# Routed rows turned in 32-blocks on VectorE instead of transposed on TensorE

## The chip, the cores and the metric

The kernel runs on one core of one Trainium2 chip. The time is that of the device for one execution, in microseconds. The program was executed three times for its times before, and once more under the profiler.

## The reference, cut to what matters

The reference is two layers, each a mixing part multiplied by the SiLU of a mixture-of-experts part, with a residual. The first layer is a RWKV recurrence with a two-expert mixture, the second a pooled attention with two shared and sixteen routed experts, four of them per token. All is float32, with T = 2048 tokens of D = 512. The change touches the second mixture:

```python
def _moe_forward(u, shared_w1, shared_b1, shared_w2, shared_b2, routed_w1, routed_b1, routed_w2, routed_b2, centroids, bias):
    flat = u.reshape(-1, d)                                   # 2048 x 512, already normalized
    h = jax.nn.relu(jnp.einsum('td,ndf->ntf', flat, shared_w1) + shared_b1[:, None, :])
    shared_out = jnp.einsum('ntf,nfd->td', h, shared_w2) + shared_b2.sum(0)
    out = flat + shared_out
    scores = jax.nn.sigmoid(flat @ centroids.T) + bias
    vals, idx = jax.lax.top_k(scores, KR)                     # KR = 4 of 16
    gating = jnp.zeros_like(scores).at[jnp.arange(T)[:, None], idx].set(vals)
    gating = gating / jnp.clip(gating.sum(-1, keepdims=True), 1e-08)

    def step(acc, ew):
        w1, b1, w2, b2, g = ew                                # 512 x 352, 352 x 512
        hj = jax.nn.relu(flat @ w1 + b1)
        yj = hj @ w2 + b2
        return (acc + yj * g[:, None], None)
    rout, _ = jax.lax.scan(step, rout0, (routed_w1, routed_b1, routed_w2, routed_b2, gating.T))
    return (out + rout).reshape(b, s, d)
```

## The kernel before

**Rows are sorted by expert through DRAM.** The normalized token rows of the second layer are kept in SBUF in `acc` ([128, 16, 544] by token tile: 512 values and 32 columns of gates and token numbers). They are written at L861 and transposed at L865 (by TensorE, with a copy on ScalarE) into `xT`, from which the routing scores `pl` (L870) come; `largest` and `chosen` pick the experts. 64 scatters on GpSimd's queue (L1043) then write every row of `acc` four times into the DRAM buffer `xs`, grouped by expert and padded to tiles of 128 rows. There are at least 64 such tiles and at most 80 (`NRT`); with these inputs 74 go through `hidden_rows`. Meanwhile the shared experts are computed (L956, L1105); their result plus the row itself (the add at L1111) is stored into two DRAM buffers, `comb[0]` and `comb[1]`, each holding half of the 512 columns.

**A routed tile has two functions.** `hidden_rows(j)` (L1657) loads the four weight pieces of the tile's expert with `load1` (L659 w1, 704 KB; L660 w2, 512 KB; L661 w3, 192 KB; L662 a bias row), from a pool of three buffers, and the tile x, [128, 544], in one DMA (L1671) that comes after all 64 scatters. The product needs the columns of x on the partitions: four TensorE transposes write `tp` in PSUM (L1678, pool `m1t` of one buffer), ScalarE copies it to `xg` (L1680), and 12 products `ph` follow (L1685), whose ReLU goes to `hT` (L942). VectorE takes the gate `g` (L1693) and the destination row `to` (L1698, L1703) from the last 32 columns of x. `down_rows(j)` (L1706) multiplies `hT` by w2, w3 (`py`, L1709, two PSUM buffers), VectorE scales by the gate to y (L1714, four buffers), and two scatter-adds on GpSimd's queue (L1717) accumulate the halves of y in `comb`.

**The loop** (L1747 to L1767) issues `hidden_rows(j)`, then pieces of the attention of the second layer as `attend_by(j)` deals them out, then `down_rows(j-1)`. All weight, x and attention loads go through SP's queue. From tile 65 on each turn stands under a test of the number of tiles. A scheduler in the framework decides the order of the instructions of each engine from this; the program's order is only its input. Attention uses the PSUM pool `aps` of three buffers (L1319). After the loop the sums are loaded from `comb` (y<-comb), put through SiLU, multiplied by attention's result, added to the residual and stored.

Of the kernel before, what the change touches and what calls it, by code (L numbers as in the profile page):

```python
# [9 lines left out]
F32 = mybir.dt.float32  # L10
I32 = mybir.dt.int32
AF = mybir.ActivationFunctionType
ALU = mybir.AluOpType
AX = mybir.AxisListType
PSUM = bass.MemoryType.PSUM
AFTER = mybir.DependencyInfo(mybir.DependencyClass.Sync, mybir.DependencyReason.DATA)

P = 128
T = 2048
D = 512  # L20
NT = T // P
NC = D // P
# [39 lines left out]
NR = 16  # L62
# [5 lines left out]
NF1 = len(FCH)  # L68
NRT = T * KR // P + NR
DX = D + 32  # L70


def bc(ap, axis, shape):
# [4 lines left out]
def tile_kernel(ctx: ExitStack, tc: tile.TileContext, a: dict):  # L78
    nc = tc.nc
# [4 lines left out]
    ident = const.tile([P, P], F32, name="ident")  # L84
# [23 lines left out]
    xs = dram.tile([NRT * P, DX], F32, name="xs")  # L108
# [66 lines left out]
    for i in range(0, NT, 2):  # L175
        xin = n0.tile([P, 2, D], F32, tag="xin", bufs=NT // 2, name="xin")
        nc.sync.dma_start(
            out=xin, in_=a["x"][i * P : (i + 2) * P, :].rearrange("(n p) d -> p n d", p=P)
# [10 lines left out]
        out=wdc, in0=gate0_w[:, :, 1], in1=gate0_w[:, :, 0], op=ALU.subtract  # L189
# [35 lines left out]
    for i in range(0, NT, 2):  # L225
# [6 lines left out]
        for j in range(2):  # L232
            xn = xin[:, j, :]
# [52 lines left out]
    own = run[:, 0, NT - 1 : NT]  # L286
# [367 lines left out]
    def load1(pool, e, pick, row):  # L654

        w1 = pool.tile([P, NC, F1], F32, tag=f"w1{e}", name="w1")
        w2 = pool.tile([P, NF1 - 1, D], F32, tag=f"w2{e}", name="w2")
        w3 = pool.tile([P, D], F32, tag=f"w3{e}", name="w3")
        nc.sync.dma_start(out=w1, in_=pick(a["w1"]))  # L659
        nc.sync.dma_start(out=w2, in_=pick(a["w2"])[:, 0 : NF1 - 1, :])  # L660
        nc.sync.dma_start(out=w3[0:last, :], in_=pick(a["w2"])[0:last, NF1 - 1, :])  # L661
        nc.sync.dma_start(out=w3[last : last + 1, :], in_=row(a["b2"]))  # L662
        return w1, w2, w3
# [184 lines left out]
    for b in range(NRB):  # L848
        rows2 = slice(b * RB, (b + 1) * RB)
        xr = tr.tile([P, n, D], F32, tag="xr", name="xr")  # L850
        nc.sync.dma_start(out=xr, in_=a["x"][rows2, :].rearrange("(n p) d -> p n d", p=P))
        i0 = b * n
        for s in range(n):
            nc.vector.tensor_tensor(
                out=xr[:, s, :], in0=xr[:, s, :], in1=acc[:, i0 + s, 0:D], op=ALU.add
            )
        nc.sync.dma_start(out=xr1[rows2, :].rearrange("(n p) d -> p n d", p=P), in_=xr)
        mv, rstd = norm_stats(xr, n)
        for s in range(n):
            i = i0 + s  # L860
            nc.vector.tensor_scalar(  # L861
                out=acc[:, i, 0:D], in0=xr[:, s, :], scalar1=mv[:, s, 0:1],
                scalar2=rstd[:, s : s + 1], op0=ALU.subtract, op1=ALU.mult,
            )
            transposed(m1y, acc[:, i, :], xT[:, :, i * P : (i + 1) * P], "py")  # L865
        if (i + 1) % (TB // P) == 0:
            t0 = i + 1 - TB // P
            pl = m1y.tile([NR, TB], F32, tag="py", name="pl")
            for c in range(NC):
                nc.tensor.matmul(  # L870
                    out=pl, lhsT=cent[:, c, :], rhs=xT[:, c, t0 * P : (i + 1) * P],
                    start=(c == 0), stop=(c == NC - 1),
                )
# [225 lines left out]
    def down_shared(tb, hT):  # L1099
        for s in range(TB // P):  # L1100
            t = tb * (TB // P) + s
            py = m1y.tile([P, D], F32, tag="py", name="py")
            for e, w in enumerate(ws):
                for f, n in enumerate(rows_of):
                    nc.tensor.matmul(  # L1105
                        out=py, lhsT=hT[0:n, e, f, s * P : (s + 1) * P],
                        rhs=down(w, f, n), start=(e == 0 and f == 0),
                        stop=(e == NS - 1 and f == NF1 - 1),
                    )
            y = m1s.tile([P, D], F32, tag="y", bufs=3, name="y")  # L1110
            nc.vector.tensor_tensor(out=y, in0=py, in1=acc[:, t, 0:D], op=ALU.add)  # L1111
            for h, c_ in enumerate(comb):
                nc.sync.dma_start(
                    out=c_[t * P : (t + 1) * P, :], in_=y[:, h * D // 2 : (h + 1) * D // 2]
                )
# [200 lines left out]
    logps.close()  # L1316


    aps = ctx.enter_context(tc.tile_pool(name="aps", bufs=3, space=PSUM))  # L1319
    QB = 256  # L1320

    def softmax(s, heads, keys, neg, wt=None, last=True):
# [206 lines left out]
    sh.close()  # L1529


    m1t = ctx.enter_context(tc.tile_pool(name="m1t", bufs=1, space=PSUM))
    aq = ctx.enter_context(tc.tile_pool(name="aq", bufs=1))
    aq2 = ctx.enter_context(tc.tile_pool(name="aq2", bufs=2))
    fin = ctx.enter_context(tc.tile_pool(name="fin", bufs=NT // 2))
# [118 lines left out]

    FIRST = 3

    def hidden_rows(j):  # L1657
        e = nc.values_load(
            tile_e[0:1, j : j + 1], engines=[mybir.EngineType.SP], min_val=0, max_val=NR - 1,
            skip_runtime_bounds_check_because="it is a count of at most NR, cut at NR - 1",  # L1660
        )
        def weights():
            return load1(
                m1w, "", lambda t: t[bass.ds(e, 1)].rearrange("e p c f -> p (e c) f"),
                lambda t: t[bass.ds(e, 1), :],
            )

        if j < FIRST:
            w = weights()
        x = m1x.tile([P, DX], F32, tag="x", bufs=4, name="x")  # L1670
        got = nc.sync.dma_start(out=x, in_=xs[j * P : (j + 1) * P, :])  # L1671
        for name in sent:
            tc.add_manual_dep(got.ins, name, AFTER, reason="any of them may hold its rows")
        if j >= FIRST:
            w = weights()
        tp = m1t.tile([P, NC, P], F32, tag="tp", name="tp")
        for c in range(NC):
            nc.tensor.transpose(tp[:, c, :], x[:, c * P : (c + 1) * P], ident)  # L1678
        xg = m1x.tile([P, NC, P], F32, tag="xg", name="xg")
        nc.scalar.copy(xg, tp)  # L1680
        hT = hts[j % len(hts)]
        for f, n in enumerate(FCH):
            ph = m1ps.tile([P, P], F32, tag="ph", name="ph")
            for c in range(NC):
                nc.tensor.matmul(  # L1685
                    out=ph[0:n, :], lhsT=up(w, f, n, c), rhs=xg[:, c, :],
                    start=(c == 0), stop=(c == NC - 1),
                )
            relu(hT[0:n, f, :], ph[0:n, :], b1t[0:n, j, f : f + 1])

        junk = m1x.tile([P, NR], F32, tag="junk", name="junk")
        g = m1x.tile([P, 1], F32, tag="g", name="g")
        nc.vector.tensor_tensor_reduce(  # L1693
            out=junk, in0=x[:, D : D + NR], in1=oh[:, j, :], scale=1.0, scalar=0.0,
            op0=ALU.mult, op1=ALU.add, accum_out=g,
        )

        nc.vector.scalar_tensor_tensor(  # L1698
            out=junk[:, 0:1], in0=x[:, D + NR + 1 : D + NR + 2], scalar=away[:, 1:2],
            in1=x[:, D + NR : D + NR + 1], op0=ALU.mult, op1=ALU.add,  # L1700
        )
        to = m1x.tile([P, 1], I32, tag="to", bufs=6, name="to")
        nc.vector.tensor_tensor(out=to, in0=junk[:, 0:1], in1=away[:, 0:1], op=ALU.add)  # L1703
        return w, hT, g, to
# [28 lines left out]
    def parts_by(j):  # L1733
# [2 lines left out]
            return (j + 1) * (PARTS - LATE) // FULL_TILES  # L1736
        return PARTS - LATE + (j - FULL_TILES) * LATE // MAYBE

    pending, taken = None, 0

    def attend_by(j):
# [5 lines left out]
    for j in range(NRT + 1):  # L1747

        with contextlib.ExitStack() as more:
            if j > FULL_TILES:  # L1750
                more.enter_context(tc.If(held > j - 1))
            made = hidden_rows(j) if j < NRT else None
            if j <= FULL_TILES:
                attend_by(j)
            if pending is not None:
                down_rows(*pending)
            pending = (j, *made) if made is not None else None
            i = j - (FULL_TILES - NT)
            if 0 <= i < NT and i % 2 == 0:
                xo = fin.tile([P, 2, D], F32, tag="xo", name="xo")  # L1760
                nc.sync.dma_start(
                    out=xo, in_=xr1[i * P : (i + 2) * P, :].rearrange("(n p) d -> p n d", p=P)
                )
                rest_of[i] = xo
        if j > FULL_TILES:
            attend_by(j)
# [119 lines left out]
```

## Time and profile before

| | us |
|---|---|
| median of three runs | 1950.14 (1944.71 to 1953.96) |
| profiled execution | 1940.83 |
| its span | 1939.1 |
| routed stage, first x load to last scatter-add landed | 1347.4 to 1877.0 |
| busy: PE, VectorE, ScalarE, GpSimd | 1857.2, 787.3, 532.9, 465.9 |

The groups of the routed stage, from the page's list of costliest groups. A row gives the line, the engine, the operation, what is written and read, the shape and the count; then the busy time in us and the mean of one in ns; then the engine's idle time just before them, and what ended most of it. PEld is the loading of the stationary operand, which lies beside the products.

```profile
L1685 PE MATMUL ph<-xg,w 128*128 128x128 f32 (+1 forms) x1776 | 214.4, 277 | 1.5 <-DMA w<-in_w_dram 1.5
L1709 PE MATMUL py<-w,ht 128*128 128x512 f32 (+1 forms) x438 | 209.1, 593 | 0.0
...
L1678 PEld LDWEIGHTS tp<-ident,x 128*128 128x128 f32 x296 | 36.7, 140 | 38.8 <-issue 21.5
```

A float32 product appears as two entries on PE: 24 for the 12 products of `ph`, 6 for the 3 of `py`.

### The profile page before, as it was taken

What the parts mean: (1) busy time and instruction counts of PE and PEld (TensorE: products, weight loads), DVE (VectorE), ACT (ScalarE), POOL (GpSimd) and SP (SyncE); (2) the same over time, 40 slices, a digit from 0 to 9 for tenths busy, and PEclk for the clock granted to TensorE, in tenths of its full rate; (3) what the DMA queues carried; (4) which work ended last, traced back from release to release, by engine and by line L of the source; (5) the groups of instructions that cost most, each with busy time, mean ns of one, the idle gap of its engine ahead of it and who ended that gap; (6) DMA issues with size and microseconds to landing.
All of it is one profiled execution on the core that took longest, in us unless ns stands there. A gap on an engine that the chain in (4) does not pass through costs nothing.

```text
span 1939.1 us, 23212 instructions
## 1 busy us (share of the span) xinstructions
PE 1857.2 (96%) x8107; PEld 1292.1 (67%) x8107; DVE 787.3 (41%) x1565; ACT 532.9 (27%) x994; POOL 465.9 (24%) x350
## 2 busy tenths in 40 slices
PE   5899999999999999999989999999999999999977
PEld 4677777787877777777533654444767777777654
DVE  8713627272634545252166544331323232223116
ACT  6212322232323232232134212221222222222223
POOL 1301212121201111020210453000344444444430
PEclk9799999999999999999999999999999999999998
DMA  7548685635654443436461553022999999999963
GB/s 250 205 144 278 205 306 178 221 108 163 197 195 141 130 131 125 157 98 233 147 227 46 174 215 114 31 95 87 313 290 316 320 311 298 292 282 265 299 148 131
DMA packets 214096, 381.35 MB, mean 197 GB/s; under 512 B 16972, under 2 KB 134476, under 8 KB 213080
## 3 DMA queue, kind: packets, MB, share of 16 engines
q1 hardware_dynamic: 183896, 332.78, 50.7%
q0 software_dynamic: 28784, 45.63, 10.7%
q10 hardware_dynamic: 1296, 1.41, 0.3%
q8 instruction: 67, 1.10, 0.2%
q14 instruction: 53, 0.43, 0.1%
HBM read 294.04 MB, written 85.72 MB: 196 GB/s over the span
## 4 chain that ended last, share of the span: by engine, by line
PE 83%; DMA 6%; DVE 3%; issue 2%; POOL 2%; ACT 2%; SPq 0%; POOLq 0%; ACTq 0%; DVEq 0%
PE pg L571 23%; PE py L593 12%; PE ph L1685 9%; PE py L1709 9%; PE proj L416 7%; PE py L1105 4%; PE ph L956 3%; PE pw L1593 2%; DMA comb<-y,to 2%; PE pq L1352 2%; PE tp L1678 1%; PE po L712 1%; PE ps L1560 1%; PE pl L870 1%; PE pw L1477 1%
## 5 line engine op out<-in xcount | busy, mean ns | idle before, releaser
L571 PE MATMUL pg<-xg,w 128*128 128x256 f32 (+1 forms) x2304 | 497.8, 369 | 3.3 <-ACT xg L563 3.3
L571 PEld LDWEIGHTS pg<-xg,w 128*128 128x128 f32 x2304 | 420.9, 191 | 95.0 <-issue 42.1
L1717 POOL DMA_INDIRECT comb<-y,to x146 | 226.9, 1554 | 300.0 <-DMA comb<-y,to 222.2
L593 PE MATMUL py<-wd,hT 128*128 128x512 f32 x544 | 256.9, 593 | 2.9 <-DVE hT L578 2.9
L1685 PEld LDWEIGHTS ph<-xg,w 128*128 128x128 f32 (+1 forms) x1776 | 201.9, 182 | 39.8 <-ACT xg L1680 32.9
L1685 PE MATMUL ph<-xg,w 128*128 128x128 f32 (+1 forms) x1776 | 214.4, 277 | 1.5 <-DMA w<-in_w_dram 1.5
L1709 PE MATMUL py<-w,ht 128*128 128x512 f32 (+1 forms) x438 | 209.1, 593 | 0.0
L578 DVE TENSOR_TENSOR hT<-sg,pg 128x256 f32<-128x256 f32 (+1 forms) x144 | 57.0, 402 | 338.4 <-ACT sg L576 338.3
L576 ACT ACTIVATE sg<-pg 128x256 f32<-128x256 f32 (+1 forms) x144 | 53.5, 372 | 419.7 <-PE pg L571 419.4
L593 PEld LDWEIGHTS py<-wd,hT 128*128 128x128 f32 x544 | 102.1, 190 | 72.2 <-issue 61.9
L1714 DVE TENSOR_SCALAR y<-py,g 128x512 f32<-128x512 f32 x73 | 54.6, 749 | 206.7 <-PE py L1709 196.1
L942 ACT ACTIVATE ht<-ph,b1t 128x128 f32<-128x128 f32 (+1 forms) x222 | 81.3, 366 | 178.9 <-PE ph L1685 161.4
L1709 PEld LDWEIGHTS py<-w,ht 128*128 128x128 f32 (+1 forms) x438 | 75.1, 191 | 49.8 <-issue 49.3
L1680 ACT COPY xg<-tp 128x512 f32<-128x512 f32 x74 | 43.4, 586 | 177.2 <-PE tp L1678 166.4
L1105 PE MATMUL py<-w,hT 128*128 128x512 f32 (+1 forms) x192 | 89.3, 596 | 0.0
L956 PE MATMUL ph<-xT,w 128*128 128x512 f32 (+1 forms) x192 | 88.0, 597 | 0.0
L1043 POOL DMA_INDIRECT xs<-acc,slot x64 | 63.1, 985 | 67.2 <-DMA xs<-acc,slot 43.5
L1352 PE MATMUL pq<-xT,wqg 128*128 128x256 f32 x224 | 56.6, 401 | 14.2 <-DVE wide L1572 9.6
L712 PE MATMUL po<-wo,yb 128*128 128x512 f32 x128 | 59.3, 620 | 9.6 <-ACT acc L721 5.5
L416 PE MATMUL proj<-xm,wr 128*128 128x256 f32 x256 | 60.9, 393 | 5.6 <-ACT v L452 5.6
L464 POOL TENSOR_TENSOR ex<-st_p,qt 128x1024 f32<-128x1024 f32 x8 | 18.3, 2288 | 193.0 <-DVE qt L463 193.0
L1678 PEld LDWEIGHTS tp<-ident,x 128*128 128x128 f32 x296 | 36.7, 140 | 38.8 <-issue 21.5
(418 smaller groups left out, 2180.9 us busy)
## 6 DMA issues: line engine op xcount, KB each, us to landing
w<-in_w_dram SPq DMA_DIRECT2D x76, 704.0 KB
w<-in_w_dram SPq DMA_DIRECT2D x76, 512.0 KB
w<-in_w_gate_dram SPq DMA_DIRECT2D x72, 512.0 KB
w<-in_w_up_dram SPq DMA_DIRECT2D x72, 512.0 KB
wd<-in_w_down_dram SPq DMA_DIRECT2D x72, 512.0 KB
xs<-zero SPq DMA_DIRECT2D x16, 1360.0 KB
x<-xs SPq DMA_DIRECT2D x74, 272.0 KB
w<-in_w_dram SPq DMA_DIRECT2D x76, 192.0 KB
```

Source lines behind the costliest of these rows:

```text
L416: nc.tensor.matmul(out=ps[:, j, :], lhsT=w_[:, c, (o0 + j) * P : (o0 + j + 1) * P], rhs=xm[:, c, :], start=(c == 0), stop=(c == NC - 1),)
L571: nc.tensor.matmul(out=pg[:, i, 0:n], lhsT=w[:, c, i * FH + f * P : i * FH + (f + 1) * P], rhs=xg[:, c, 0:n], start=(c == 0), stop=(c == N ...
L593: nc.tensor.matmul(out=p, lhsT=hT[:, u * P : (u + 1) * P], rhs=wd[:, f, :], start=first_, stop=last_,)
L712: nc.tensor.matmul(out=po, lhsT=yb[:, c, s * P : (s + 1) * P], rhs=wo[:, c, :], start=(c == 0), stop=(c == NC - 1),)
L942: nc.scalar.activation(dst, src, AF.Relu, bias=b)
L956: nc.tensor.matmul(out=ph[0:n, :], lhsT=up(w, f, n, c), rhs=xT[:, c, cols], start=(c == 0), stop=(c == NC - 1),)
L1043: ins = nc.gpsimd.indirect_dma_start(out=xs, out_offset=bass.IndirectOffsetOnAxis(ap=slot[:, i, k : k + 1], axis=0), in_=acc[:, i, :], in_ ...
L1105: nc.tensor.matmul(out=py, lhsT=hT[0:n, e, f, s * P : (s + 1) * P], rhs=down(w, f, n), start=(e == 0 and f == 0), stop=(e == NS - 1 and f ...
L1352: nc.tensor.matmul(out=pq[:, j, :], lhsT=w[:, c, w0 : w0 + P], rhs=xT[:, c, tc0], start=(c == 0), stop=(c == NC - 1),)
L1685: nc.tensor.matmul(out=ph[0:n, :], lhsT=up(w, f, n, c), rhs=xg[:, c, :], start=(c == 0), stop=(c == NC - 1),)
L1709: nc.tensor.matmul(out=py, lhsT=hT[0:n, f, :], rhs=down(w, f, n), start=(f == 0), stop=(f == NF1 - 1),)
L1717: nc.gpsimd.indirect_dma_start(out=c_, out_offset=bass.IndirectOffsetOnAxis(ap=to, axis=0), in_=y[:, h * D // 2 : (h + 1) * D // 2], in_of ...
```

## The change

The transposition of a routed tile on TensorE, its PSUM buffer and ScalarE's copy are replaced by one VectorE transpose of 32 x 32 blocks. That instruction turns each of the 4 x 16 blocks of a [128, 512] tile within its 32 partitions; it doesn't move a block to other partitions. So the blocks are put on their partitions by the load: the quarter q (32 partitions) of the tile gets, from each of four groups of 32 rows, the column blocks that belong to q. For each of these to be one run of 128 values in DRAM, the columns of the rows are stored in another order: 512 columns as (c q k), with k of 32, are kept in `acc` and `xs` as (q c k).

- At L861 the row goes to a tile `xn` of its own (two buffers), is transposed from there, and ScalarE copies it reordered to `acc`. The shared experts' add reads `acc` through a permuted view.
- `weights(j)` and `rows_in(j)` are split from `hidden_rows(j)`. `rows_in` loads x in four DMAs of 32 partitions each and the last 32 columns as `own` in a fifth, and turns them. It is called one tile ahead; the weights of three tiles are called before the first.
- `aps` has four buffers instead of three, `m1t` is gone.

```diff
@@ the rows of the second layer @@
+            xn = tr.tile([P, D], F32, tag="xn", bufs=2, name="xn")
             nc.vector.tensor_scalar(
-                out=acc[:, i, 0:D], in0=xr[:, s, :], scalar1=mv[:, s, 0:1],
+                out=xn, in0=xr[:, s, :], scalar1=mv[:, s, 0:1],
                 scalar2=rstd[:, s : s + 1], op0=ALU.subtract, op1=ALU.mult,
             )
-            transposed(m1y, acc[:, i, :], xT[:, :, i * P : (i + 1) * P], "py")
+            transposed(m1y, xn, xT[:, :, i * P : (i + 1) * P], "py")
+            nc.scalar.copy(
+                acc[:, i, 0:D].rearrange("p (c q k) -> p q c k", q=NB, k=BL),
+                xn.rearrange("p (c q k) -> p q c k", q=NB, k=BL),
+            )
...
-            nc.vector.tensor_tensor(out=y, in0=py, in1=acc[:, t, 0:D], op=ALU.add)
+            nc.vector.tensor_tensor(
+                out=y.rearrange("p (c q k) -> p c q k", q=NB, k=BL),
+                in0=py.rearrange("p (c q k) -> p c q k", q=NB, k=BL),
+                in1=acc[:, t, 0:D].rearrange("p (q c k) -> p c q k", q=NB, k=BL), op=ALU.add,
+            )
...
-    aps = ctx.enter_context(tc.tile_pool(name="aps", bufs=3, space=PSUM))
+    aps = ctx.enter_context(tc.tile_pool(name="aps", bufs=4, space=PSUM))
...
-    m1t = ctx.enter_context(tc.tile_pool(name="m1t", bufs=1, space=PSUM))
...
-    def hidden_rows(j):
+    def weights(j):
...
+        return load1(
+            m1w, "", lambda t: t[bass.ds(e, 1)].rearrange("e p c f -> p (e c) f"),
+            lambda t: t[bass.ds(e, 1), :],
+        )
...
-        x = m1x.tile([P, DX], F32, tag="x", bufs=4, name="x")
-        got = nc.sync.dma_start(out=x, in_=xs[j * P : (j + 1) * P, :])
...
-        tp = m1t.tile([P, NC, P], F32, tag="tp", name="tp")
-        for c in range(NC):
-            nc.tensor.transpose(tp[:, c, :], x[:, c * P : (c + 1) * P], ident)
+    def rows_in(j):
+        x = m1x.tile([P, NB, NC, BL], F32, tag="x", bufs=4, name="x")
+        own = m1x.tile([P, DX - D], F32, tag="own", bufs=4, name="own")
+        mine = xs[j * P : (j + 1) * P, :]
+        loads = [
+            nc.sync.dma_start(
+                out=x[q * BL : (q + 1) * BL].rearrange("p b c k -> p b (c k)"),
+                in_=mine[:, q * P : (q + 1) * P].rearrange("(b r) k -> r b k", r=BL),
+            )
+            for q in range(NB)
+        ]
+        loads.append(nc.sync.dma_start(out=own, in_=mine[:, D:]))
...
         xg = m1x.tile([P, NC, P], F32, tag="xg", name="xg")
-        nc.scalar.copy(xg, tp)
+        nc.vector.transpose(xg.rearrange("p c (b r) -> p b c r", r=BL), x)
+        return xg, own
+
+    def hidden_rows(j, w, xg, own):
...
+    ready = [weights(j) for j in range(FIRST)]
+    rows = rows_in(0)
...
-            made = hidden_rows(j) if j < NRT else None
+            made = None
+            if j < NRT:
+                mine, rows = rows, rows_in(j + 1) if j + 1 < NRT else None
+                made = hidden_rows(j, ready.pop(0) if ready else weights(j), *mine)
```

`NB` is 4 and `BL` is 32. The gate and the destination read `own` where they read the last columns of x before.

More of the change, by code (lines that the diff above doesn't have):

```diff
@@ L70 @@
 DX = D + 32
+NB = 4
+BL = P // NB
 def bc(ap, axis, shape):
@@ L860, in tile_kernel @@
             i = i0 + s
+            xn = tr.tile([P, D], F32, tag="xn", bufs=2, name="xn")
             nc.vector.tensor_scalar(
-                out=acc[:, i, 0:D], in0=xr[:, s, :], scalar1=mv[:, s, 0:1],
+                out=xn, in0=xr[:, s, :], scalar1=mv[:, s, 0:1],
                 scalar2=rstd[:, s : s + 1], op0=ALU.subtract, op1=ALU.mult,
             )
-            transposed(m1y, acc[:, i, :], xT[:, :, i * P : (i + 1) * P], "py")
+            transposed(m1y, xn, xT[:, :, i * P : (i + 1) * P], "py")
+            nc.scalar.copy(
+                acc[:, i, 0:D].rearrange("p (q c k) -> p q c k", q=NB, k=BL),
+                xn.rearrange("p (c q k) -> p q c k", q=NB, k=BL),
+            )
         if (i + 1) % (TB // P) == 0:
@@ L1661, in hidden_rows @@
         )
[L1662 to L1665, printed above, removed]
-            )
-        if j < FIRST:
-            w = weights()
-        x = m1x.tile([P, DX], F32, tag="x", bufs=4, name="x")
-        got = nc.sync.dma_start(out=x, in_=xs[j * P : (j + 1) * P, :])
[L1672 to L1675, printed above, removed]
-        tp = m1t.tile([P, NC, P], F32, tag="tp", name="tp")
-        for c in range(NC):
-            nc.tensor.transpose(tp[:, c, :], x[:, c * P : (c + 1) * P], ident)
+        return load1(
[10 more added lines that the diff above has]
+                in_=mine[:, q * P : (q + 1) * P].rearrange("(b r) k -> r b k", r=BL),
+            )
+            for q in range(NB)
+        ]
+        loads.append(nc.sync.dma_start(out=own, in_=mine[:, D:]))
+        for got in loads:
+            for name in sent:
+                tc.add_manual_dep(got.ins, name, AFTER, reason="any of them may hold its rows")
         xg = m1x.tile([P, NC, P], F32, tag="xg", name="xg")
-        nc.scalar.copy(xg, tp)
+        nc.vector.transpose(xg.rearrange("p c (b r) -> p b c r", r=BL), x)
+        return xg, own
+    def hidden_rows(j, w, xg, own):
         hT = hts[j % len(hts)]
@@ L1693, in hidden_rows @@
         nc.vector.tensor_tensor_reduce(
-            out=junk, in0=x[:, D : D + NR], in1=oh[:, j, :], scale=1.0, scalar=0.0,
+            out=junk, in0=own[:, 0:NR], in1=oh[:, j, :], scale=1.0, scalar=0.0,
             op0=ALU.mult, op1=ALU.add, accum_out=g,
@@ L1698, in hidden_rows @@
         nc.vector.scalar_tensor_tensor(
-            out=junk[:, 0:1], in0=x[:, D + NR + 1 : D + NR + 2], scalar=away[:, 1:2],
-            in1=x[:, D + NR : D + NR + 1], op0=ALU.mult, op1=ALU.add,
+            out=junk[:, 0:1], in0=own[:, NR + 1 : NR + 2], scalar=away[:, 1:2],
+            in1=own[:, NR : NR + 1], op0=ALU.mult, op1=ALU.add,
         )
```

## The prediction, on record before the changed kernel ran

> **What bounds the kernel now.** I read the busy shares by slice first, then the same by windows of 50 us over the routed stage, then its waits, then the packets. The busy tenths put the stage in the second half of the span, where PE and DMA both stand at 9:
>
> ```profile
> span 1939.1 us, 23212 instructions
> ...
> PE   5899999999999999999989999999999999999977
> ...
> DMA  7548685635654443436461553022999999999963
> ...
> L1717 POOL DMA_INDIRECT comb<-y,to x146 | 226.9, 1554 | 300.0 <-DMA comb<-y,to 222.2
> ...
> L1680 ACT COPY xg<-tp 128x512 f32<-128x512 f32 x74 | 43.4, 586 | 177.2 <-PE tp L1678 166.4
> ```
>
> In the windows (PE, PEld, DVE, ACT, POOL busy; then clock, DMA share, GB/s) PE has no idle time at all, and the DMA share is also about 1; DVE and ACT are idle three quarters of the time:
>
> ```profile
> 1500.00:1550.00 50.00, 50.00 (x276) 35.15 (x275) 12.99 (x45) 13.82 (x33) 21.29 (x14) 1.00 1.05 323
> ...
> 1750.00:1800.00 50.00, 50.00 (x264) 34.25 (x263) 13.31 (x44) 13.54 (x31) 23.58 (x16) 1.00 0.90 254
> ```
>
> So two resources are near their limits. Which is the nearer? The waits from 1400 to 1860 say: the weight loads on SP wait for PE to release buffers, hardly for transfers: in the order of limits PE comes first. But the scatter-adds wait for one another throughout, and VectorE waits for them:
>
> ```profile
> SPq L660 <- PE py L1709: 166.7, 57, 6.6
> ...
> SPq L660 <- DMA w<-in_w_dram: 6.6, 7, 1.5
> ```
>
> ```profile
> POOL comb L1717 <- DMA comb<-y,to: 201.3, 87, 5.5
> ...
> DVE to L1703 <- DMA comb<-y,to: 101.5, 30, 6.7
> ```
>
> Reading single instructions, the first product of the stage starts at 1355.5, the last y ends at 1859.4, and the last scatter-add lands at 1877.0: the accumulation runs 17 us behind the products. Where no attention work lies between (tiles 64 to 70) the y follow each other 5.81 us apart; the mean over tiles 6 to 63 is 7.07.
>
> **The change, part by part.**
>
> 1. *Four transposes and their copy go.* Each PE transpose costs 0.107 us when they run together, 0.43 us a tile, with some 0.13 us of entry and a slower first product of the group: 5.81 − (2.66 ph + 2.58 py) = 0.57 us. Over 74 tiles PE is relieved of **42 us**. ACT loses 74 × 0.586 = 43 us, worth nothing: it is busy 27%.
>
> 2. *VectorE gets 75 block transposes* of 128x512 f32. No such row is in the trace; the nearest are whole-tile VectorE operations, 0.69 us (L1111, L839) and 0.749 us (L1714). I bound it by 0.6 and 1.2 us and take 0.75: 56 us, on an engine with 35 us free of each 50. The transposition of tile j+2 follows y(j) in VectorE's order. Its wait is for x(j+2), issued about two tiles, over 10 us, before; loads of x landed 6.27 us (median) after issue. So it costs 0; if the cover fails, what is queued behind it is to(j+2) and y(j+1), hence the scatter-add, and py's two PSUM buffers, which stop PE one tile later.
>
> 3. *One x load becomes four of 64 KB and one of 16 KB.* Packets: 128 of 2176 B become 512 of 512 B and 128 of 128 B, with 64 more semaphore writes. In the trace's packet records 2176 B takes 88 ns, 512 B 27 ns (the xnt loads, L245), 128 B 13 ns, a semaphore 9 ns. So 11.3 us of engine time become 13.8 + 1.7 + 0.6 = 16.1: **+0.30 us a tile** over 16 engines. All of a tile's DMAs together now need 93.9/16 = 5.87 us (weights 56.1, x 11.5, scatter-adds 26.3), so 6.17 after. With some 17 us of attention's loads, use from 1350 to 1850 is 440/500 = 0.88, at best 0.93 held over longer stretches and 0.97 in single ones of 20 us. (The DMA share counts queueing too, and so reaches 1.05.)
>
> Here a rule speaks against the change. The Trainium skill, page "SBUF — State Buffer", section "Door 1: The DMA port swizzle", says that a range of 32 partitions reaches 8 of 16 ports, and gives 189 GB/s at 1 MiB against 328 for 128 partitions. Each quarter writes 32 partitions. By the row 64 KB take 128 × 27/16 = 0.22 us; by the rule's limit for 8 ports, 218 GB/s, 0.30 us, which is +0.33 us a tile again, 24 us in all. The row is of 128-partition loads, so it can't exclude this. But other transfers are in flight that use the other ports, so I take the row, and keep the rule for the slow end.
>
> Another, in "DMA: Bandwidth & Descriptors", section "Measured", would have a 64 KB transfer at 0.95 us, and so 3.8 us for the four: 9 us a tile, 660 us in the stage. That is the price of one transfer by itself; here loads overlap (x lands 6.27 us after issue while a tile takes 7), so I don't sum them.
>
> 4. *SP issues nine DMAs a tile in place of five.* A two-dimensional load takes SP 0.36 us, one with 512-byte runs 0.53 (L245: 512/532/639): x goes from 0.36 to some 2.4 us, the tile from about 3.4 with its registers to 5.4, just under the tile's 7. More serious: in the built program each SP DMA waits for the eighth before it, so up to 1.6 tiles can be in flight before and 0.9 after; w1 of a tile waits for w2 of the tile before, and `own` for its group's w1. With landings of 5.3 to 6.3 us this gives a cycle of 6.0 to 6.3 us a tile, close under the mean of 7.07, but above the 5.24 that PE would need where it has no attention work.
>
> 5. *Attention is bunched.* In the changed order on PE attention's work lies in five clumps (11, 14, 15, 16 and 22 us of PE, at tiles 2-6, 14-18, 27-32, 40-45, 53-58) and not evenly. In the gaps PE asks for a tile every 5.24 us, DMA can give one every 6.17/0.93 = 6.6: PE waits there, and in the clumps DMA can run ahead by three weight buffers only.
>
> 6. *Start of the stage.* Three weight sets are now issued up front, and the fourth quarter of x(0) waits its turn for a lane until w1 of tile 1 has landed: first product about 7 us later (1363). Attention work of 9.3 us moved before it covers most of PE's loss; DMA loses some 3 us. I take +3 (−2 to +8).
>
> 7. *Reordered copies* (L870 after): ACT gets 16 of some 0.59 us (the 128x512 copy, L1680), 9.4 us, in the stretch from 1020 to 1051 where PE waits for ACT: four groups of transposes, xT copy, pl 3.6 us, lg copy, 7.3 us apart. xn's two buffers make VectorE wait for those copies, and interleave square roots and sigmoids, so some four more table loads (1.28 us in the trace). At least 0, if hidden beside pl; at most 9.4 + 5.1 = 14. I take +6, since PE is busy 35.4 of 40 us there and half the copies must find no gap. The permuted VectorE add (L1111) has 4.46 us of idle before it; aps's fourth buffer serves an engine with no idle time. Both 0.
>
> 8. *Tail.* Attention left after the last tile: 33.7 us of PE instead of 41.7, but after the last scatter-add the sums still have to be loaded, gated and stored; the chain of waits at the end alternates between these loads (1884 to 1895) and attention's pw products (1902 to 1932): −2 (−8 to 0).
>
> **The sum.** Stage: 440 + 74 × 0.30 = 462 us of DMA work; at 0.93 use 497 us, at 0.90 514, at 0.88 526, against 500 now; PE's need falls to 458. I take 0.90, above the mean since buffers come free earlier, below the best since fewer transfers can be in flight: **+14**. With +6, +3 and −2 that is +21 on the profiled execution's 1940.8, so 1962; this run lay 9 below the median 1950.1, so a median of about **1970**.
>
> **Rivals.**
> - *DMA follows PE* (0.22). If the transfers go at 0.97, as in single stretches, the stage takes 476 us, −24 + 7: 1933. It decides from a use of 0.957 (483 us) on. For it: 0.88 is set by PE's demand now, SP hardly ever waits for transfers, and the scatter interval falls to 4.5 to 5.7 us once the weights stop. Against: scatter-adds take 9.1 to 9.9 us an interval in the first tiles, when loads run unchecked.
> - *Given back exactly* (0.13). 0.93 use, the copies hidden: −3 + 3 − 2, 1948. PE then shows 30 to 40 us of idle time and the end doesn't move.
> - *Quarters at half width or starved lanes* (0.17): +24 us of work, at 0.90 use +27 on mine, 1997; at 0.88 2010. Then SP waits for loads of w and x at every tile.
> - *Forecast* (0.48): the stage bound by transfers, 1955 to 1990.
>
> **How the numbers follow.** Runs lie within 0.5% of their median, 10 us, so less can't be told from no change. Faster is the first rival, 0.22; same the second, 0.13; the forecast and the third are slower, 0.65. The range, 1932 to 2006, takes in the first rival's value and most of the third's; outside are a better use than 0.97 and the worst of the half width.
>
> **What would show it.** PE idle in the windows of the stage, some 50 us, in the gaps of attention; ph waiting for w or the scatter-adds for each other; y spaced 6.3 to 6.6 us in those gaps; SP's waits turned from PE py to DMA; VectorE's transposes 0.6 to 1.2 us with no wait for x; 512 B packets at 27 ns (37 means half width); xs's scatter 6 us later. It is wrong if PE keeps 100% busy in the stage with y 5.3 us apart (the first rival), or if VectorE waits for x.

## The result and the profile after

The changed kernel takes **1977.97 us** (median of four, 1973.62 to 1983.58), the kernel before 1949.62 beside it: a ratio of 1.0161, 95% interval 1.0132 to 1.0191. It is slower by some 28 us. The forecast was 1970, from 1932 to 2006.

The two profiled executions differ by 36.9 us of span (1976.0 against 1939.1). From single instructions of both traces, in order of time:

| | before | after | difference |
|---|---|---|---|
| first load of x | 1347.4 | 1350.5 | +3.1 |
| from there to the first product | 8.1 | 23.4 | +15.3 |
| first product to the start of the last y | 503.9 | 527.0 | +23.1 |
| from there to the end | 79.7 | 75.0 | −4.7 |

PE's own time between the first product and the last y shows the exchange: the 31.2 us of the transposes are gone, and 45.5 us of idle time have come where there was none; the entries of `ph` are busy for 6.3 us longer and those of attention for 2.0.

The busy tenths of the changed kernel, in 40 slices. PE has lost its unbroken row of nines in the routed stage, from slice 29 on; DMA has kept it:

```profile
span 1976.0 us, 23010 instructions
...
PE   5899999999999999999889999998989898989775
...
DMA  7557786635462534446522651024999999999974
```

Windows of 50 us in the stage (PE, PEld, DVE, ACT, POOL busy with counts; then the granted TensorE clock, the DMA share, GB/s):

```profile
1500.00:1550.00 50.00, 47.12 (x267) 34.35 (x266) 13.10 (x43) 8.79 (x24) 21.95 (x15) 1.00 1.04 280
1550.00:1600.00 50.00, 43.02 (x214) 31.98 (x215) 17.82 (x58) 7.79 (x21) 20.29 (x14) 0.93 0.99 267
...
1700.00:1750.00 50.00, 45.79 (x240) 32.74 (x238) 13.91 (x44) 8.78 (x24) 20.51 (x14) 0.93 1.06 297
```

PE is now idle in every one of the eleven from 1350 to 1900, 52 us in all; before had 18, none of it between 1400 and 1850. The transfer engines are as full as before (share about 1) but move less: in the nine windows from 1400 to 1850 279 GB/s in the mean, and 297 before. SP's waits from 1400 to 1850 (us, times, longest) have changed sides; before, its largest row was the w2 load waiting 166.7 us for PE:

```profile
SPq L661 <- DMA w<-in_w_dram: 53.3, 47, 3.1
SPq L1691 <- DMA w<-in_w_dram: 41.5, 50, 3.1
SPq L1685 <- DMA w<-in_w_dram: 12.9, 13, 1.7
SPq L663 <- PE py L1728: 4.3, 9, 1.6
```

L661 is w1, L1685 a quarter of x, L1691 `own`. All three wait for weights to land. The groups of the page that answer to those shown of before:

```profile
L1704 PE MATMUL ph<-xg,w 128*128 128x128 f32 (+1 forms) x1776 | 218.7, 282 | 35.1 <-DMA w<-in_w_dram 26.4
L1728 PE MATMUL py<-w,ht 128*128 128x512 f32 (+1 forms) x438 | 200.7, 594 | 1.2 <-DMA w<-in_w_dram 1.2
...
L1733 DVE TENSOR_SCALAR y<-py,g 128x512 f32<-128x512 f32 x73 | 54.8, 750 | 282.5 <-PE py L1728 282.4
...
L1696 DVE STREAM_TRANSPOSE xg<-x 128x512 f32<-128x512 f32 x75 | 52.9, 706 | 64.6 <-DMA x<-xs 55.7
```

PE waited 1.5 us before `ph` and waits 35.1 now, most of it for weights. The block transpose takes 0.706 us, and 55.7 us of VectorE's idle time before it are waits for x.

### The profile page after: what moved, and what is told of

Same layout as the page of the kernel before. It is cut to its first block, busy times and chain, and to the rows that moved or that the text cites. A ratio compares the mean times of both kernels' runs of the same rounds, so it can differ in the third digit from the quotient of the medians.

```text
span 1976.0 us, 23010 instructions
## 1 busy us (share of the span) xinstructions
PE 1839.1 (93%) x7811; PEld 1277.6 (65%) x7811; DVE 821.5 (42%) x1640; ACT 495.5 (25%) x936; POOL 467.1 (24%) x350
## 4 chain that ended last, share of the span: by engine, by line
PE 75%; DMA 13%; DVE 3%; issue 3%; ACT 3%; POOL 2%; SPq 1%; ACTq 0%; POOLq 0%; DVEq 0%
PE pg L573 23%; PE py L595 11%; PE ph L1704 7%; PE proj L418 7%; PE py L1728 5%; DMA w<-in_w_dram 4%; PE py L1113 4%; DMA comb<-y,to 4%; PE ph L964 3%; PE pq L1364 2%; PE pw L1604 2%; PE po L714 1%; PE ps L1571 1%; PE pl L878 1%; PE pw L1489 1%
## 5 line engine op out<-in xcount | busy, mean ns | idle before, releaser
L1704 PEld LDWEIGHTS ph<-xg,w 128*128 128x128 f32 (+1 forms) x1776 | 211.8, 188 | 68.6 <-DVE to L1722 24.0
L1704 PE MATMUL ph<-xg,w 128*128 128x128 f32 (+1 forms) x1776 | 218.7, 282 | 35.1 <-DMA w<-in_w_dram 26.4
L1728 PE MATMUL py<-w,ht 128*128 128x512 f32 (+1 forms) x438 | 200.7, 594 | 1.2 <-DMA w<-in_w_dram 1.2
L1696 DVE STREAM_TRANSPOSE xg<-x 128x512 f32<-128x512 f32 x75 | 52.9, 706 | 64.6 <-DMA x<-xs 55.7
L547 POOL DMA_INDIRECT xr<-in_x_dram,tok x17 | 23.2, 1366 | 160.4 <-PE tp L562 143.3
L418 PE MATMUL proj<-xm,wv 128*128 128x256 f32 x256 | 60.6, 392 | 0.0
```

The lines of the kernel that those rows point to most:

```text
L418: nc.tensor.matmul(out=ps[:, j, :], lhsT=w_[:, c, (o0 + j) * P : (o0 + j + 1) * P], rhs=xm[:, c, :], start=(c == 0), stop=(c == NC - 1),)
L1704: nc.tensor.matmul(out=ph[0:n, :], lhsT=up(w, f, n, c), rhs=xg[:, c, :], start=(c == 0), stop=(c == NC - 1),)
L1728: nc.tensor.matmul(out=py, lhsT=hT[0:n, f, :], rhs=down(w, f, n), start=(f == 0), stop=(f == NF1 - 1),)
```

## The experiments

Two theories, both of them within "the transfers bind": the **packets** theory, that the 512-byte packets of x cost engine time as the prediction summed them, and the **half-width** theory, that what costs is that each quarter lands on 32 partitions. A third, the **slots** theory, has nine DMAs a tile starving a queue in which each waits for the eighth before.

A fourth stood in the prediction as "attention is bunched", and no run was made for it alone. The framework's scheduler orders PE's work anew for each program. Counted from the traces, a piece of attention lies at every second or third tile in before; in the changed kernel seven or eight tiles in a row have none, in four_full three to five, and in one_512 and one_2048 hardly any is without. So a difference between two runs can be the edit's or that of the order that came with it. The order is nearly the same in one_512, one_2048 and one_512_two; in before, before_two and half_before; and in the changed kernel, after_two and, behind the first tiles, own_once and late_weights.

The kernel before was run beside each: its median was 1948.72 for the first four kernels, 1947.32 for the next four, 1943.42 for the last four. So ratios are compared, not times alone.

### One load of x in place of four, with 512-byte and with 2048-byte runs

```diff
-            nc.sync.dma_start(
-                out=x[q * BL : (q + 1) * BL].rearrange("p b c k -> p b (c k)"),
-                in_=mine[:, q * P : (q + 1) * P].rearrange("(b r) k -> r b k", r=BL),
-            )
-            for q in range(NB)
+            nc.sync.dma_start(          # one_512
+                out=x.rearrange("p b c k -> p b (c k)"),
+                in_=xs[at : at + NB * P, 0:P].rearrange("(b r) k -> r b k", r=P),
+            )
...
+            nc.sync.dma_start(out=x.rearrange("p b c k -> p (b c k)"), in_=mine[:, 0:D])  # one_2048
```

> The changed kernel, but x of a tile is loaded by one DMA over 128 partitions in place of four over 32; the 512 packets of 512 bytes stay (they are taken from the first 128 columns of four neighbouring tiles, so the routed rows are not the right ones; the amount of work is the same). Six DMAs a tile in place of nine. Packets theory (only the engine time of the 512-byte packets counts): as the changed kernel, 1978 +- 6, mean of a 512-byte packet 38 ns as there. Half-width theory (a quarter writes 32 partitions and so crowds the SBUF side): the mean packet falls from 38 to 28-30 ns, 4-5 us of engine time a tile, some 0.3 us over 16 engines, 1955 to 1962. Slots theory (each DMA of SP waits for the eighth before it, nine a tile starve the queue): SP's waits for w disappear and the time falls by 15 to 25 with the packet's mean unchanged.

> As one_512, but each partition gets its 512 values as one run of 2048 bytes (own row, not regrouped, so again not the right rows; same amount of work). Packets theory: 512 x 27 ns become 128 x 84 ns, 3.1 us of engine time a tile, 0.2 us over 16 engines, and more if the 38 ns seen count (8.7 us, 0.54 us a tile): 1940 to 1963. Slots theory: the same time as one_512 within 5 us, since both have six DMAs. Half-width theory: 0 to 10 below one_512.

Measured: one_512 1953.59 us, ratio 1.0028 (1.0009 to 1.0048); one_2048 1955.63, ratio 1.0029 (1.0013 to 1.0046). Four times as many packets, the same order on PE, and no difference: the packets theory falls. One load over 128 partitions in place of four over 32, with the even order of attention that comes with it, takes nearly all of the loss away. In one_512 no product waits for weights:

```profile
L1704 PE MATMUL ph<-xg,w 128*128 128x128 f32 (+1 forms) x1776 | 212.7, 277 | 2.3 <-DVE t L1376 2.3
```

The mean 512-byte packet between 1400 and 1800 is 38 ns in the changed kernel (median 28) and 32 in one_512 (median 27). This is no support for the half-width theory: own_once below loads quarters too and is as slow as the changed kernel, and its mean is 33 (median 27).

### Four loads of full width

Which of the two did it, the number or the width? The same four loads, each over 128 partitions:

```diff
-                out=x[q * BL : (q + 1) * BL].rearrange("p b c k -> p b (c k)"),
-                in_=mine[:, q * P : (q + 1) * P].rearrange("(b r) k -> r b k", r=BL),
+                out=x[:, q].rearrange("p c k -> p (c k)"),
+                in_=xs[(at + q) * P : (at + q + 1) * P, 0:P],
```

> The changed kernel, with four x loads of 64 KB and `own` in a fifth as there (nine DMAs a tile), but each of the four covers 128 partitions with one 512-byte run in place of 32 partitions with four (the runs are the first columns of four neighbouring tiles, so the routed rows are not the right ones; the amount of work is the same). Half-width theory: what the quarters cost is that they land on 32 partitions; as one_512, 1954 +- 6, mean of a 512-byte packet near 32 ns. Number-of-DMAs theory (nine in eight slots, SP's issues): as the changed kernel, 1978 +- 6, with SP waiting for w as there (about 110 us).

Measured: 1960.4 us, ratio 1.0071 (1.0049 to 1.0093). Of the 24 us between the changed kernel and one_512, some 17 are gone and some 7 are left (the intervals of four_full and one_512 just miss each other). The 17 can't all be put down to the width. In SP's order the fourth load of the first tile now stands before the weights and no longer behind twelve of their DMAs, so the first product comes 7.1 us after the first load of x and not 23.4; and attention is less bunched. A transfer of 64 KB lands little sooner: in the median 5.1 us after its issue over 128 partitions, 5.5 over 32 (last semaphore update on its slot, 1400 to 1800). And SP's waits for weights are still there:

```profile
SPq L661 <- DMA w<-in_w_dram: 40.4, 49, 1.9
SPq L1692 <- DMA w<-in_w_dram: 36.3, 44, 1.9
SPq L1686 <- DMA w<-in_w_dram: 17.2, 14, 2.6
```

94 us against 108 over the same stretch. PE too still waits for weights, 20.6 us between first product and last y, 27.6 in the changed kernel.

### One DMA a tile fewer, in quarters

```diff
-        own = m1x.tile([P, DX - D], F32, tag="own", bufs=4, name="own")
+        own = own_all[:, j, :]
...
-        loads.append(nc.sync.dma_start(out=own, in_=mine[:, D:]))
...
+    for a0, a1 in ((0, 8), (8, NRT)):
+        got = nc.sync.dma_start(
+            out=own_all[:, a0:a1, :],
+            in_=xs[a0 * P : a1 * P, D : D + NR + 2].rearrange("(t p) k -> p t k", p=P),
+        )
```

> The changed kernel, but the last columns of all tiles are loaded by two DMAs at the start of the stage; eight DMAs a tile in place of nine, and w1 then waits for the w1 of the tile before and no more for w2. x is still loaded in quarters. Slots theory: SP's waits for w (113 us over the stage) fall below 40, the time by 10 to 20: 1958 to 1968. Packets and half-width theory: within 5 of the changed kernel, 1973 to 1983.

Measured: 1983.21, ratio 1.0155 (1.0114 to 1.0197), the same as the changed kernel. But it is not the same wait. PE's waits from 1375 to 1870, in the changed kernel and then in own_once:

```profile
PE ph L1704 <- DMA w<-in_w_dram: 23.8, 17, 3.1
PE ps L1577 <- DVE qg L1377: 6.2, 4, 2.2
...
PE ps L1577 <- DVE qg L1377: 26.9, 8, 9.9
...
PE ph L1703 <- DMA w<-in_w_dram: 3.1, 4, 1.0
```

With eight DMAs in place of nine, the quarters kept, the weights come in time. What holds PE now is attention's `qg` on VectorE. It stands there behind `to`, which waited for scatter-adds 53.2 us in 16 waits; the changed kernel has no such wait. (At 1478.1 `to` had waited 7.0 us; `qg` came after it, and PE, at 1480.0, had stood idle for 9.9.) So the slots theory is right about PE's waits for weights; the time doesn't follow, because the chain of scatter-adds (below) stands next in line.

### Quarters alone, in the kernel before

```diff
-        got = nc.sync.dma_start(out=x, in_=xs[j * P : (j + 1) * P, :])
+        for q in range(4):
+            got = nc.sync.dma_start(
+                out=x[q * 32 : (q + 1) * 32, :],
+                in_=xs[j * P + q * 32 : j * P + (q + 1) * 32, :],
+            )
```

> The kernel before, x of a tile loaded by four DMAs of 32 rows on 32 partitions, each row one run of 2176 bytes as before; eight DMAs a tile in place of five, and nothing else changed. Half-width theory: the quarters alone push the stage from PE's bound to the transfers': 1960 to 1972. Packets or order theory (quarters harmless, the 512-byte runs or attention's place cost): within 6 of before, 1943 to 1955.

Measured: 1974.13 us, ratio 1.0145 (1.0109 to 1.0181), as slow as the changed kernel. This looks like the sharpest run, but it isn't the kernel before with quarters and nothing else: the scheduler has ordered PE's work anew. Attention is bunched as in the changed kernel, and the transposes have moved. PE in before, then in split_rows:

```profile
1603.59 1.88 PE L1709 MATMUL py<-w,ht 128*128 128x512 f32 x4
1605.31 0.60 PE L1678 MATMUL tp<-ident,x 128*128 128x128 f32 x4
1605.74 1.02 PE L1709 MATMUL py<-w,ht 128*128 128x512 f32 x2
1606.64 2.92 PE L1685 MATMUL ph<-xg,w 128*128 128x128 f32 x24
...
1457.99 2.74 PE L1713 MATMUL py<-w,ht 128*128 128x512 f32 x6
1460.57 0.60 PE L1682 MATMUL tp<-ident,x 128*128 128x128 f32 x4
1461.90 2.92 PE L1689 MATMUL ph<-xg,w 128*128 128x128 f32 x24 [0.73 <-ACT xg L1684]
```

In before two products of `py` cover ScalarE's copy of the transposes; in split_rows `ph` follows the transposes at once and waits 0.73 us for that copy, at nearly every tile without attention. These tiles come 6.7 us apart, before's 5.8. The page has it as PE's idle time before `ph`:

```profile
L1689 PE MATMUL ph<-xg,w 128*128 128x128 f32 (+1 forms) x1776 | 214.4, 277 | 33.3 <-ACT xg L1684 30.0
```

PE never waits for weights here. So this run shows no cost of the quarters' transfer: four of 68 KB a tile, eight DMAs in all, keep up with a tile every 6.7 us. Their packets are longer, though: the same 2176 bytes take 105 ns in the median between 1400 and 1800 and 88 in before (means 128 and 94).

The runs side by side, PE's idle time between the first product and the last y in us, by what ended it:

| | DMAs a tile | x on | idle | weights | largest other |
|---|---|---|---|---|---|
| changed kernel | 9 | 32 partitions | 45.5 | 27.6 | 6.2 `qg` of VectorE |
| late_weights (below) | 9 | 32 | 44.5 | 27.3 | 6.3 `qg` |
| four_full | 9 | 128 | 40.5 | 20.6 | 6.3 `mx` of VectorE |
| own_once | 8 | 32 | 40.3 | 8.5 | 26.9 `qg` |
| split_rows | 8 | 32 | 35.9 | 0 | 29.3 ScalarE's copy |
| one_512 | 6 | 128 | 26.0 | 0 | 10.8 `qg` |

The waits for weights follow the number of DMAs more closely than the width. What the width costs by itself was not found: no run changes it and keeps both the number and the order.

### What PE's relief is worth where transfers don't bind

In both kernels odd tiles use the weights of the even tile before, so half of the weight loads are left out:

```diff
+        if j % 2:
+            return kept[0]
-        return load1(
+        kept[0] = load1(
...
+        return kept[0]
```

> The changed kernel with every second tile's weights left out (odd tiles use those of the even tile before, so theirs are mostly the wrong expert's only at a change of expert; weight loads are halved). DMA work falls by 28 us of engine time a tile, 1.75 us over 16 engines. If transfers are the bound of the stage, PE's need now sets it, 5.24 us a tile with 80 us of attention, and the last y comes some 45 to 60 us earlier: 1915 to 1930. If the order on PE or VectorE's waits hold it, 1955 or more. If the scatter-adds' chain holds it, their interval stays at 6.5 to 7 us and the time at 1945 to 1960.

> The kernel before with every second tile's weights left out, as in half_after. PE is its bound already, so less transfer work gives little: 1935 to 1945, y 5.81 us apart between attention work. Against half_after (1910) that would measure what the change gives PE where transfers don't bind, predicted at 42 us less some 10 to 15 at the start: 25 to 35. If before too gains 20 or more, transfers had a share in its bound.

Measured: half_after 1910.17, ratio 0.9801 (0.9752 to 0.9850); half_before 1926.41, ratio 0.9907 (0.9872 to 0.9942). In the traces the stretch from the first product to the last y is 504.3 us in half_before, as in before (503.9), and 463.7 in half_after: **40.6 us less**, with 1.3 us of idle time on PE. The transposes are not all of that. They are 31.2 us of it, quicker entries of `ph` 3.0, and 7.6 are attention's work that half_after does before or behind the stretch. Between the medians only 16 us remain, where 25 to 35 were expected: half_after reaches its first load of x 6.5 us later, takes 9.7 more from there to the first product and 11.1 more behind the last y. half_before, 9 us below what was expected of it, gains nearly all behind the stage, where it ends 68.0 us after the last y begins and before 79.7: its scatter-adds land 6 us behind the last y and no longer 17.

### The chain of scatter-adds

one_512 has one x load of full width and PE freed of the transposes, and still isn't faster than before. Its chain of waits (start us, us, what) says why. In before this stretch is PE, and the scatter-adds make 2% of the whole chain; here they make 17%, one after another:

```profile
1490.23 6.99 DMA comb<-y,to
1497.49 5.86 DMA comb<-y,to
1503.62 7.25 DMA comb<-y,to
1511.14 7.52 DMA comb<-y,to
1518.93 6.85 DMA comb<-y,to
1526.05 6.95 DMA comb<-y,to
```

Some 7.2 us from one to the next, one for each tile. So the accumulator in DRAM was doubled: even and odd tiles add to different ones, of full width, and the two are added at the end.

```diff
-    comb = [dram.tile([T + P, D // 2], F32, name=f"comb{h}") for h in range(2)]
+    comb = [dram.tile([T + P, D], F32, name=f"comb{h}") for h in range(2)]
...
-        for h, c_ in enumerate(comb):
-            nc.gpsimd.indirect_dma_start(
-                out=c_, out_offset=bass.IndirectOffsetOnAxis(ap=to, axis=0),
-                in_=y[:, h * D // 2 : (h + 1) * D // 2], in_offset=None, compute_op=ALU.add,
-            )
+        nc.gpsimd.indirect_dma_start(
+            out=comb[j % 2], out_offset=bass.IndirectOffsetOnAxis(ap=to, axis=0),
+            in_=y, in_offset=None, compute_op=ALU.add,
+        )
...
+        nc.gpsimd.tensor_tensor(out=y, in0=y, in1=z, op=ALU.add)
```

The second is filled with zeros beside `xs`, and z is its load at the end.

> one_512 (not the right rows), with two accumulators of full width in DRAM, one for even and one for odd tiles, added at the end, so a scatter-add waits for the last but one and not for the last. Chain theory: what takes PE's relief back in one_512 is that each scatter-add waits for the one before (its chain of waits is comb after comb, some 7.1 us a tile); with two chains PE or the transfers set the stage: the last y comes 10 to 25 us earlier than in one_512, the time 1925 to 1942. DMA theory (the engines are simply full, 0.91 of undisturbed use): the last y moves less than 5 us and the time 0 to 10, since only the lag at the end goes: 1944 to 1954.

> The kernel before, with two accumulators as in one_512_two and nothing else. PE is busy without a gap in its stage, so both theories let the last y stay at 1860 +- 3; the scatter-adds then end 6 to 9 us behind it and not 17, and the end gains 0 to 10, less some 2 for the added loads and additions: 1938 to 1950.

> The changed kernel, right rows and quarters included, with two accumulators of full width as in one_512_two. If what the quarters cost is the transfers' own time (x at 38 ns a packet, all 16 engines full), the stage stays near 7.3 us a tile, w is waited for as in the changed kernel, and the time gains only what the end gains in the kernel before, 10 to 15: 1960 to 1968. If the quarters only lengthen the scatter-adds' chain, taking the chain away frees them as in one_512_two: 6.6 to 6.9 us a tile, 1920 to 1935.

| | us | ratio | 95% interval | first product to last y |
|---|---|---|---|---|
| one_512_two | 1912.73 | 0.9823 | 0.9778 to 0.9869 | 475.3 (one_512: 510.9) |
| before_two | 1935.40 | 0.9929 | 0.9910 to 0.9949 | 504.5 (before: 503.9) |
| after_two | 2010.21 | 1.0351 | 1.0295 to 1.0406 | 549.4 (after: 527.0) |

one_512_two shows the chain theory right, and by more than expected: with full-width loads the chain was the next bound. A second thing changed with it, half as many scatter-adds with 2048-byte packets in place of 1024. From the median packets (178 and 102 ns) that spares an estimated 0.2 us a tile over 16 engines; the tiles come 0.54 us closer (7.17 to 6.63 between tiles 10 and 60), so it can't be the whole. PE is idle for 3.0 us in the stretch and no longer 26.0.

one_512_two against before_two is also the best measure of the relief, with all weights loaded: 1.1% or some 21 us less, the intervals apart, though with rows that aren't the tile's own. In before_two the stage stays as it was, since PE sets it; 4.3 us are gained behind the last y and 5.5 before the first load of x, in one profile each. With right rows, before_two is faster than both kernels of the comparison, by 0.7% against before; it has nothing of the change in it.

after_two missed both of its expectations: it is 32 us *slower* than the changed kernel. Its scatter-adds no longer wait for one another but for y, and its transfers are slower yet, the mean 512-byte packet 41 ns and the median 36, and PE waits 35.5 us for weights and not 27.6. Two rows of its windows:

```profile
1550.00:1600.00 50.00, 41.40 (x192) 29.67 (x192) 18.11 (x58) 7.79 (x21) 9.31 (x6) 0.90 0.96 268
1600.00:1650.00 50.00, 47.36 (x271) 35.76 (x271) 12.72 (x42) 8.42 (x23) 10.86 (x7) 1.00 0.97 251
```

Full-width scatter-adds do no harm in before_two or one_512_two, so it is their meeting with the changed kernel's nine DMAs a tile, four of them quarters, that costs. Why was not found, and this stays open.

### The start

```diff
-    ready = [weights(j) for j in range(FIRST)]
+    ready = []
```

> The changed kernel, but the first three tiles' weights are not called before the first rows; each is called in its own turn. Start theory: the 15 us by which the first product is later than before, beyond the stage's own delay, come from x(0) waiting behind twelve weight DMAs; the first product comes at 1362-1366 and not 1374, and the time falls by 4 to 8 (the rest was attention work brought forward): 1970 to 1974. If the start is paid back by attention work or by DMA: 1978 +- 4.

> after_two with each tile's weights called in its own turn, as in late_weights, so the first product comes some 12 us earlier. By late_weights (4 less than the changed kernel) 3 to 6 below after_two. If the start is paid back in the stage when transfers are full, within 3 of it.

Measured: late_weights 1974.22, ratio 1.0131 (1.0105 to 1.0158), its first product at 1362.0 in place of 1373.9; after_two_late 2005.25, ratio 1.0293 (1.0247 to 1.0340), 5 below after_two with intervals that overlap. Of the 12 us at the start about 4 remain at the end, with intervals that overlap. The stretch from the first product to the last y grows to 531.4: attention's work that stood before the first product is done within the stage.

## Why the prediction was right, and where its steps were not

The direction and the place were right, and of the mechanism the main part: PE was freed, stands idle for some 50 us in the stage, and the largest share of that (27.6 of 45.5 us) is for weights that haven't landed. That +21 was forecast and 28 measured between medians, 37 between profiles, is in part luck: the terms were off both ways.

- **Four transposes and their copy go, 42 us.** Right in kind, too large: 34 in half_after against half_before (31.2 of transposes, 3.0 of quicker `ph`). PE's busy time in the page fell by 18 only (1857.2 to 1839.1), since `ph` and attention took longer.
- **VectorE's transposes.** 0.706 us for the 0.75 taken. But "It costs 0", with the load of x two tiles ahead, failed, and a wait of VectorE for x was named as a sign of being wrong: there are 18, of 55.7 us. SP issues the quarters late, behind the weights in the same eight slots: of the load groups after 1540, one has its quarters issued from 1549 to 1550 and its transpose, which waited 5.04 us, at 1556.55. PE's weight load for `ph` waited 34 us for VectorE from 1375 to 1870.
- **x in quarters, +0.30 us a tile.** It was summed from the sizes of packets, and the sizes are without effect (one_512, one_2048). What the quarters cost in its place stays open. The packets don't show the half width: the sign named was 37 ns for 27, a median, and the median is 28. The rule that the prediction kept for the slow end, of the Trainium skill's page "SBUF — State Buffer", section "Door 1: The DMA port swizzle", that 32 partitions reach half of the ports, is neither shown nor excluded: no trace tells the ports, and split_rows, which was to decide it, lost its time elsewhere. That the total came near is because 0.90 of use was assumed for other reasons. By the same sum it is 0.84 to 0.89 in the windows from 1400 to 1850.
- **Nine DMAs in eight slots.** Called "more serious", and given no term of its own. SP's waits turned as said, 47 to 50 times for some 60 tiles, which was the sign of the rival "starved lanes"; and with eight DMAs PE's waits for weights fall from 27.6 us to 8.5 (own_once). So the forecast's time came with a good part of that rival's mechanism. What the slots cost in time was not isolated.
- **Attention bunched.** The gaps were there, about 52 us of idle PE, as said, and in one_512, where attention is spread evenly, PE doesn't wait for weights. But the tiles in the gaps don't come 6.3 to 6.6 us apart: after a clump four or five follow at PE's own 5.2, from buffers filled in the clump, and then some at 6 to 8.
- **Start.** +3 was forecast, 15 measured between first load and first product, of which a test gives back 4. **Reordered copies:** +6 forecast, +3.1 between the two profiles; in the mean the first load of x comes at 1351.9 in six kernels with the copies and at 1346.9 in three without, +5.0. **Tail:** −2 forecast; from the last scatter-add's landing to the end −3.1 (62.1 to 59.0).
- **The rivals.** "DMA follows PE" at 0.97 didn't happen with quarters; with a load of full width and two accumulators PE set the pace, at 1912.7, below the 1933 forecast for it. The prediction read the waits of scatter-adds for each other as a sign of full transfers. They are a bound by themselves: PE, the transfers and a chain lay within a few per cent of each other, and the sum had no term for the chain.

## What to carry to other kernels

Before splitting a load so that an engine finds its data laid out, count the DMAs of a tile against the slots of their queue. Here nine in eight slots left PE waiting for weights, with quarters and with full-width loads alike, while 512-byte runs in one load cost nothing against 2048-byte ones.

When PE is 100% busy, ask what stands next before relieving it. Here the weights' slots and a chain of dependent transfers did; with both out of the way the relief was worth 1.1%. Compare the chain's interval (7.2 us here) with the tile's period, and leave half of the loads out once: that run shows whether the transfers are what PE waits for.

And where a scheduler orders the engines' work, look at that order before reading a run as the cost of its edit. split_rows has the loss of the changed kernel to a few us, and most of it is a copy that two products used to cover.

## What the runs showed that was not expected

- Means of packets tell little about width. The 2176-byte packets of x take 128 ns in split_rows and 94 in before, but 102 in before_two and 114 in half_before, on 128 partitions as well; their median is 105 in split_rows and 88 in those three.
- Idle PE can cost twice. Before, the granted clock is 1.00 in every window from 1350 to 1850; after, it is 0.93 in three windows and 0.97 in two. The mean entry of `ph` grew from 277 to 282 ns. half_after, where PE is never idle from 1400 to 1600, has 1.00 there again. But split_rows, with up to 4.6 us of idle time in a window, has 1.00 in all nine from 1400 to 1850: no wait of PE is longer than 0.73 us there. In the changed kernel the clock's record falls to half for 3.4 or 6.8 us, four times in that stretch, each beside a wait of 1.8 to 3.1 us. The Trainium skill's page "TensorE: Matmul & The Clock Gate", section "HAM oscillation — how this bites in real kernels", tells of waits for transfers that bring the clock down, and names gaps above some 3.4 us; the waits here are shorter.
- The scatter-adds, freed of their chain, gave 41 us with one x load a tile (one_512_two) and cost 32 with four quarters (after_two).
